# Aggregating and summing layer 1 of a graph network by two groups of four graphs instead of one

## The chip, the cores and the metric

The kernel runs on one core of one Trainium2 chip. Time is measured on the device in microseconds (us), as the median of several runs. Beside these runs there is one execution that the hardware profiler recorded; rows, timelines and waits below come from that one.

Five engines work side by side, each with its own queue of instructions: TensorE (PE in the profile, with its weight loads shown as PEld), VectorE (DVE), ScalarE (ACT), GpSimd (POOL) and SyncE (SP), which here issues transfers only. PSUM is the memory that TensorE writes; VectorE and ScalarE read from it.

## The reference, cut to what matters

128 graphs of 128 nodes with 256 features pass through two layers. Layer 0 is a large gated network (convolutions by a Fourier method, messages between neighbours, gates). Layer 1 looks at the first 25 nodes of each graph only, in five overlapping groups of nodes, 53 rows in all:

```
x = x + layer0(relu(layernorm(x)), adj)
h = relu(layernorm(x))
fused = 0
for g, idx in enumerate(GROUPS):          # sizes 25, 9, 7, 6, 6
    A = adj[:, idx][:, :, idx] + I
    N = D^-1/2 A D^-1/2                   # D: row sums of A
    y = relu(N @ (h[:, idx] @ W1[g]) + b1[g])
    z = relu(N @ (y @ W2[g]) + b2[g])     # this second aggregation is what the change touches
    fused[:, idx] += softmax(fusion_w)[g] * z
x = x + fused
```

Everything is computed in fp32.

## The kernel before, in words

**Layer 0 and its place.** After two batches of preparation, the gates of layer 0 are computed for 32 groups q of four graphs by `stage_c` (products on line 758, some with their own accumulation banks in the pool `pgat`). Each group's result is turned back by VectorE (lines 921 to 939), written to HBM by GpSimd (L941), and read again by `fetch`: the first 32 nodes of the four graphs become `x1`, 128 rows of 256.

**Layer 1 and its tiling.** Layer 1 works in eight blocks of 16 graphs, each block four groups of four (`SB` = 16, `GB` = 4, `QS` = 4). The 53 rows of a graph are padded to 64 (`RP`), so that two graphs fill 128 partitions. For each block:

- `rows` normalizes `x1` of each group.
- `prepare` builds the normalized adjacency `ac` for the 16 graphs (128 partitions: two graphs of 64; eight pairs), and spreads it by one product, `pr4` on L1074, to a mask `r4`. This product stands in the kernel before and is not changed.
- `block` first aggregates (`py`, L1094), then runs the two dense products of the five node groups (`first`, L1111, and `second`, L1120), which end in `yz`, features by rows.
- Then comes the tail of the block, three small functions, each called once for every group q of four graphs. `turn(q)` transposes `yz` back on TensorE into a PSUM bank `pz` (L1142) and ScalarE copies it to `zt`, rows by features for two pairs of graphs (L1146). `gather(q)` aggregates: four products of 64x64 weights with 256 columns, one for each of four graphs, each in its own quadrant of the TensorE array (L1154), into two PSUM tiles `pg2`; VectorE adds the bias to each (L1157), and ScalarE applies relu to both at once (L1158). `fuse(q)` sums the five node groups by two products with 64 weight columns, one on each half of the array's columns (L1164), VectorE adds the result to `x1` (L1166), and the 32 nodes of four graphs are stored. In blocks 0 to 6, GpSimd stores a group with one transfer (L1169). In the last block, each graph has a transfer of its own, 16 in all, issued by SP, but for two of the last group that ScalarE issues (L1173).

**What sets the order.** The order in which instructions enter the queues is written by a planner at build time (`Order`, `Lane`). Programs are Python generators. A step yields two numbers: the time that it is thought to cost, and a pause before the program may go on. Lanes with less work done for their weight go first, if their step is due; otherwise the first lane that is due goes. `stage_c` is one lane; `prepare` and `block` of layer 1 together are another of weight 0.2, two programs at a time. A block begins once its own `prepare` has ended (`P_DONE`) and the gathers of the block before have been issued (`B1_DONE`). In the last products of each layer 0 group the steps of `stage_c` yield a pause of 0.2.

**Buffers.** The pool `ptmp` has five PSUM banks under the tag "tmp" for all short-lived products: those of layer 1 and some of layer 0. A bank holds 512 fp32 columns; a tile of 256 takes a whole bank too. `zt` has four buffers of 2 x 256.

Of the kernel before, what the change touches and what calls it, by code (L numbers as in the profile page):

```python
# [9 lines left out]
FP = mybir.dt.float32  # L10
AF = mybir.ActivationFunctionType
# [4 lines left out]
B, N, D = 128, 128, 256  # L16
# [3 lines left out]
P = 128  # L20
GB = 4
# [9 lines left out]
SB = 16  # L31
QS = SB // GB
NBLK = B // SB
# [7 lines left out]
RP = 64  # L41
WIDE = 32
# [168 lines left out]
def kernel(ctx: ExitStack, tc: tile.TileContext, x, adj, consts, vecs, w_se, conv1_w,  # L211
                    conv2_w, w_msg, b_msg, w_ih, w_hh, W1, W2, b2, fusion_w, out):
    nc = tc.nc
# [7 lines left out]
    ptmp = ctx.enter_context(tc.tile_pool(name="ptmp", bufs=5, space=PSUM))  # L221
# [19 lines left out]
    def v(name, i=None):  # L241
        a, b = VAT[name]
        return vec[:, a:b] if i is None else vec[:, a + i:a + i + 1]
# [17 lines left out]
    s2w = cp.tile([P, 2 * WIDE], FP, name="s2w")  # L261
# [106 lines left out]
    lab, turn = ExitStack(), []  # L368
# [625 lines left out]
    def load_w1(n):  # L994

        if n < NBLK * NG:
            S["w1", n] = S["pool"].tile([P, 2, HID], FP, tag="w1", name=f"w1_{n}", bufs=2)
            nc.sync.dma_start(out=S["w1", n], in_=W1[n % NG].rearrange("(k p) o -> p k o", p=P))
# [83 lines left out]
    def block(blk):  # L1082
        while not (blk in P_DONE and blk - 1 in B1_DONE):
            yield 0.0, 0.5
        pool, yz, b2row = S["pool"], S["yz"], S["b2row"]
        w2, ac, r4 = S["w2"], S["ac"][blk % 2], S["r4"][blk % 2]

        for q in range(QS):
            while blk * QS + q not in R_DONE:
                yield 0.0, 0.5  # L1090
            x1h = S.pop(("x1h", blk * QS + q))
            py = ptmp.tile([P, 2, GB, NR], FP, tag="tmp", name=f"py{blk}_{q}")
            for cc in range(2):
                nc.tensor.matmul(py[:, cc], x1h[:, cc * P:(cc + 1) * P],  # L1094
                                 r4[:, q].rearrange("p j r -> p (j r)"), start=True, stop=True)
            nc.vector.tensor_copy(yz[:, 0, q * GB:(q + 1) * GB, :NR], py[:, 0])  # L1096
            nc.scalar.activation(yz[:, 1, q * GB:(q + 1) * GB, :NR], py[:, 1], AF.Copy)
            PY_DONE.add(blk * QS + q)
            yield 0.75, 0.0 if q < QS - 1 else 2.4

        hs = {}

        def first(g):
            n, o = SIZES[g], OFFS[g]
            w1 = S.pop(("w1", blk * NG + g))
            hh = hs[g] = pool.tile([P, 4, SB, n], FP, tag="hh0" if g == 0 else "hh",
                                   name=f"hh{blk}_{g}", bufs=1 if g == 0 else 2)
            for m in range(4):
                ph = ptmp.tile([P, SB, n], FP, tag="tmp", name=f"ph1{blk}_{g}_{m}")
                for k in range(2):  # L1110
                    nc.tensor.matmul(ph, w1[:, k, m * P:(m + 1) * P],  # L1111
                                     yz[:, k, :, o:o + n], start=(k == 0), stop=(k == 1))
                nc.scalar.activation(hh[:, m], ph, AF.Relu, bias=v("b1", g * 4 + m))  # L1113

        def second(g):
            n, o = SIZES[g], OFFS[g]
            for cc in range(2):
                pz = ptmp.tile([P, SB, n], FP, tag="tmp", name=f"pz1{blk}_{g}_{cc}")
                for m in range(4):
                    nc.tensor.matmul(pz, w2[:, g, m, cc * P:(cc + 1) * P], hs[g][:, m],  # L1120
                                     start=(m == 0), stop=(m == 3))
                nc.vector.tensor_copy(yz[:, cc, :, o:o + n], pz)

        for g in range(NG + 1):
            if g < NG:
                first(g)
                yield 5.5 if g == 0 else 1.95, 0.0
            if g:
                second(g - 1)
                yield 5.5 if g == 1 else 1.95, 0.0 if g < NG else 1.0  # L1130
            if g < NG:
                load_w1(blk * NG + g + 2)
        x1 = X1[blk]

        zts = {}

        def turn(q):
            pz = ptmp.tile([P, 2, D], FP, tag="tmp", name=f"pzt{blk}_{q}")
            for a in range(2):
                for cc in range(2):  # L1140
                    b0 = q * GB + 2 * a
                    nc.tensor.transpose(  # L1142
                        pz[:, a, cc * P:(cc + 1) * P],
                        yz[:, cc, b0:b0 + 2, :].rearrange("p s r -> p (s r)"), ident)
            zt = zts[q] = pool.tile([P, 2, D], FP, tag="zt", name=f"zt{blk}_{q}", bufs=4)
            nc.scalar.activation(zt, pz, AF.Copy)  # L1146

        def gather(q):
            zt = zts[q]
            pg2 = [ptmp.tile([P, D], FP, tag="tmp", name=f"pg2{blk}_{q}_{s}") for s in range(2)]  # L1150
            for a in range(2):
                for s in range(2):
                    rows = slice(s * RP, (s + 1) * RP)
                    nc.tensor.matmul(pg2[s][a * RP:(a + 1) * RP], ac[rows, 2 * q + a],  # L1154
                                     zt[rows, a], start=True, stop=True)
            for s in range(2):
                nc.vector.tensor_add(zt[:, s], pg2[s], b2row)  # L1157
            nc.scalar.activation(zt, zt, AF.Relu)  # L1158

        def fuse(q):  # L1160
            zt = zts.pop(q)
            pf = ptmp.tile([P, D], FP, tag="tmp", name=f"pfu{blk}_{q}")
            for s in range(2):
                nc.tensor.matmul(pf[s * 2 * WIDE:(s + 1) * 2 * WIDE], s2w, zt[:, s],  # L1164
                                 start=True, stop=True)
            nc.vector.tensor_add(x1[:, q], x1[:, q], pf)  # L1166
            b0 = blk * SB + q * GB
            if blk < NBLK - 1:
                nc.gpsimd.dma_start(out=out[b0:b0 + GB, :WIDE], in_=x1[:, q])  # L1169
                return  # L1170
            for j in range(GB):
                eng = nc.scalar if q == QS - 1 and j % 2 else nc.sync
                eng.dma_start(out=out[b0 + j, :WIDE], in_=x1[j * WIDE:(j + 1) * WIDE, q])  # L1173

        for what, q in ((turn, 0), (turn, 1), (turn, 2), (gather, 0), (turn, 3), (gather, 1),
                        (gather, 2), (fuse, 0), (gather, 3), (fuse, 1), (fuse, 2), (fuse, 3)):
            what(q)
            if (what, q) == (gather, QS - 1):
                B1_DONE.add(blk)
            yield {turn: 0.45, gather: 0.5, fuse: 0.5}[what], 0.5  # L1180
        F_DONE.add(blk)


# [23 lines left out]
    loads = Lane([stage_n(q) for q in range(NQ)])  # L1207
    groups = Lane([stage_c(q) for q in range(NQ)], ahead=2)
    second = [setup_1()] + [part(blk) for blk in range(NBLK) for part in (prepare, block)]
    beside.weight = 0.5  # L1210
    order.run(loads, groups, beside, Lane([fetch(q) for q in range(NQ)], ahead=2),
# [43 lines left out]
```

## Time and profile before

| | us |
|---|---|
| median of 3 runs | 1995.26 (1993.5 to 1996.35) |
| profiled execution, its own time | 1999.49 |
| its span, first to last instruction | 1997.7 |
| TensorE busy in the span | 1950.6 |
| VectorE busy | 1349.5 |
| ScalarE busy | 683.2 |
| gather, L1154: 256 records of 128 products, TensorE | 21.4 |
| fuse, L1164: 128 records of 64 products, TensorE | 20.8 |
| bias, L1157: 64 adds of 128x256, VectorE, each | 0.418 |
| relu, L1158: 32 of 128x512, ScalarE, each | 0.630 |
| copy of a turn, L1146: 32 of 128x512, ScalarE, each | 0.593 |
| sum into x1, L1166: 32 adds of 128x256, VectorE, each | 0.417 |
| an add of 128x512 with a broadcast row, L428 (layer 0), each | 0.687 |

How to read it: an fp32 product leaves two records, each with a weight load. Matmuls are pipelined, so a record's duration overlaps the next one's; what a product costs the queue is the distance between starts. A timeline line has the start, the time from the first start to the last end of the instructions merged in it, the engine, the line of the kernel, the operation, output and input, the shape, the count, and in brackets idle time of the engine ahead of it with what ended it.

Layer 1's blocks 0 to 5 run beside layer 0, from about 898 us on. The products of layer 0 end at 1904; its last results are turned until 1917. Blocks 6 and 7 run after that.

### The profile page before, as it was taken

The page shows a single profiled execution, that of the slowest core. Times are in us where ns is not written, and L with a number is a line of the kernel's source. Part 1 is how long each engine was busy: PE and PEld are TensorE (multiplying, and loading weights), DVE is VectorE, ACT ScalarE, POOL GpSimd, SP SyncE. Part 2 cuts the span into 40 slices and gives each one's busy share as a digit, 9 for nine tenths or more (in the row PEclk, how much of TensorE's full clock was granted, in tenths as well). Part 3 has the DMA queues.
Part 4 walks back from the last instruction along what each step waited for, and adds up shares of the span by engine and source line. Part 5 has one row for each costly group of instructions (what it writes and reads, how often), then busy time and mean ns, then how long its engine had stood idle before and what let it go on. Part 6 is the DMA issues. An engine that isn't in the chain of part 4 may idle for free.

```text
span 1997.7 us, 33167 instructions
## 1 busy us (share of the span) xinstructions
PE 1950.6 (98%) x12486; PEld 1610.6 (81%) x12486; DVE 1349.5 (68%) x3042; ACT 683.2 (34%) x1547; POOL 650.1 (33%) x898
## 2 busy tenths in 40 slices
PE   7999999999999999999999999999999999999998
PEld 5667888889888888878778878878888888887865
DVE  6775445875433566885885887778678867886652
ACT  3664222444222344222323322232323322322233
POOL 3553665333665111240321233122221321322320
PEclk9999999999999999999999999999999999999999
DMA  9998778654877643542434343443433533433332
GB/s 207 300 283 274 259 265 283 204 164 152 274 254 254 193 127 106 162 106 80 116 95 108 111 111 84 114 109 95 120 110 82 127 105 98 109 101 98 77 90 57
DMA packets 184106, 302.89 MB, mean 152 GB/s; under 512 B 28501, under 2 KB 131994, under 8 KB 183690
## 3 DMA queue, kind: packets, MB, share of 16 engines
q1 hardware_dynamic: 138762, 168.82, 29.1%
q0 software_dynamic: 44800, 131.66, 23.1%
q8 instruction: 99, 1.62, 0.4%
q14 instruction: 61, 0.50, 0.1%
q10 hardware_dynamic: 384, 0.28, 0.1%
HBM read 204.13 MB, written 109.05 MB: 157 GB/s over the span
## 4 chain that ended last, share of the span: by engine, by line
PE 86%; DVE 6%; DMA 4%; issue 1%; ACT 1%; POOL 1%; SPq 0%; DVEq 0%; POOLq 0%; ACTq 0%
PE p L758 40%; PE pa L534 7%; PE ph L1111 5%; PE pm L645 5%; PE pz L1120 5%; PE pc L425 4%; PE pb L534 3%; PE pf L436 3%; PE px L671 3%; PE pi L715 2%; PE pw L480 1%; PE ph L414 1%; PE py L1094 1%; PE pg L1154 1%; PE pse L629 1%
## 5 line engine op out<-in xcount | busy, mean ns | idle before, releaser
L941 POOL DMA_DIRECT2D x1d<-xt x128 | 101.1, 815 | 418.8 <-DVE xt L939 418.4
L840 POOL DMA_DIRECT2D xt<-in_x x128 | 100.2, 790 | 175.4 <-DMA x1d<-xt 168.3
L566 DVE SCALAR_TENSOR_TENSOR y<-pa,kk 128x512 f32<-128x512 f32 x78 | 53.8, 690 | 151.4 <-ACT kk L565 151.4
L534 PE MATMUL pa<-wf,X 128*128 128x256 f32 x640 | 152.2, 381 | 0.0
L758 PE MATMUL p<-th,wrz 128*128 128x256 f32 x512 | 135.4, 387 | 0.0
L758 PE MATMUL p<-tm,wrz 128*128 128x256 f32 x512 | 131.9, 380 | 0.0
L758 PE MATMUL p<-tc,wrz 128*128 128x256 f32 x512 | 131.4, 379 | 0.0
L534 PEld LDWEIGHTS pa<-wf,X 128*128 128x128 f32 x640 | 118.1, 190 | 16.2 <-issue 2.0
L425 PE MATMUL pc<-c1w,hTa 128*128 128x256 f32 x512 | 121.0, 382 | 1.2 <-ACT hTa L416 1.2
L645 PE MATMUL pm<-wmsg,hT 128*128 128x256 f32 x512 | 121.5, 382 | 0.0
L758 PEld LDWEIGHTS p<-th,wrz 128*128 128x128 f32 x512 | 95.1, 191 | 18.7 <-issue 6.3
L1111 PE MATMUL ph<-yz,w 128*128 128x96 f32 (+3 forms) x640 | 107.9, 322 | 1.8 <-DVE yz L1096 1.3
L758 PEld LDWEIGHTS p<-tm,wrz 128*128 128x128 f32 x512 | 97.8, 191 | 13.5
L425 PEld LDWEIGHTS pc<-c1w,hTa 128*128 128x128 f32 x512 | 94.0, 190 | 18.1 <-DVE h L428 4.8
L758 PEld LDWEIGHTS p<-tc,wrz 128*128 128x128 f32 x512 | 97.3, 190 | 14.0 <-issue 1.0
L645 PEld LDWEIGHTS pm<-wmsg,hT 128*128 128x128 f32 x512 | 95.8, 190 | 15.2 <-ACT kk L565 1.4
L727 ACT ACTIVATE xc<-xc,t_bn 128x256 f32<-128x256 f32 x128 | 58.1, 501 | 145.9 <-DVE xc L724 145.9
L1120 PE MATMUL pz<-hh,w 128*128 128x96 f32 (+3 forms) x640 | 107.3, 322 | 0.0
L1111 PEld LDWEIGHTS ph<-yz,w 128*128 128x128 f32 x640 | 86.8, 190 | 22.9 <-issue 15.0
L1113 ACT ACTIVATE hh<-ph,vec 128x96 f32<-128x96 f32 (+3 forms) x160 | 63.2, 401 | 120.5 <-PE ph L1111 111.7
L1120 PEld LDWEIGHTS pz<-hh,w 128*128 128x128 f32 x640 | 86.3, 191 | 17.6
L758 PE MATMUL p<-hTc,wrz 128*128 128x256 f32 x384 | 99.2, 381 | 1.1 <-DVE z L832 1.1
(207 smaller groups left out, 4433.6 us busy)
## 6 DMA issues: line engine op xcount, KB each, us to landing
wf<-wfd SPq DMA_DIRECT2D x160, 256.0 KB
wfd<-ws POOLq DMA_DIRECT2D x64, 320.0 KB, 9.0
yd<-y POOLq DMA_DIRECT2D x80, 256.0 KB, 4.1
yt<-yd SPq DMA_DIRECT2D x64, 320.0 KB
w<-in_W SPq DMA_DIRECT2D x40, 512.0 KB
xa<-in_x SPq DMA_DIRECT2D x128, 128.0 KB
hTd<-hTa POOLq DMA_DIRECT2D x32, 512.0 KB, 6.7
hT<-hTd SPq DMA_DIRECT2D x32, 512.0 KB
```

The lines of the kernel that those rows point to most:

```text
L425: nc.tensor.matmul(pc[:, i], hT[:, k, (2 * h + i) * N:(2 * h + i + 1) * N], c1w[:, k], start=(k == 0), stop=(k == 1))
L436: nc.tensor.matmul(pf[:, i, :F * NB], h1[:, 2 * h + i, k * P:(k + 1) * P], fwd, start=True, stop=True)
L534: nc.tensor.matmul(ps, xk(k), WF[f][:, k, s], start=(k == 0), stop=(k == 1))
L645: nc.tensor.matmul(pm[:, i], hT[:, k, j * N:(j + 1) * N], LATE["wmsg"][:, k], start=(k == 0), stop=(k == 1))
L671: nc.tensor.matmul(px[:, dc, i], msgs[h][:, i, dc * P:(dc + 1) * P], aT[:, 2 * h + i], start=True, stop=True)
L727: nc.scalar.activation(xc[:, co, s], xc[:, co, s], AF.Relu, bias=sft["bn2"][:, co:co + 1])
L758: nc.tensor.matmul(ps[:, m], w[:, i, k, m * P:(m + 1) * P], factor(i, x, t), start=first and j == 0, stop=last and j == len(n) - 1, skip_g ...
L840: nc.gpsimd.dma_start(out=xt[a * WIDE:(a + 1) * WIDE].rearrange("p b d c -> p (b d) c"), in_=slices(x[q * GB:(q + 1) * GB])[a])
L941: nc.gpsimd.dma_start(out=slices(x1d[q])[a], in_=xt[a * WIDE:(a + 1) * WIDE].rearrange("p b d c -> p (b d) c"))
L1111: nc.tensor.matmul(ph, w1[:, k, m * P:(m + 1) * P], yz[:, k, :, o:o + n], start=(k == 0), stop=(k == 1))
L1113: nc.scalar.activation(hh[:, m], ph, AF.Relu, bias=v("b1", g * 4 + m))
L1120: nc.tensor.matmul(pz, w2[:, g, m, cc * P:(cc + 1) * P], hs[g][:, m], start=(m == 0), stop=(m == 3))
```

## The change

`turn` is still called for each group of four graphs, but writes into a `zt` that holds two groups (two buffers of 2 x 2 x 256). `gather` and `fuse` now take two groups, h: `gather` issues eight quadrant products one after the other into two full PSUM banks, then for each of the two banks an add and a relu of 128x512. `fuse` issues two products of 512 columns, one add to `x1`, and the two groups' stores. The order becomes turn 0, 1, 2, gather 0, turn 3, gather 1, fuse 0, fuse 1. The step of a gather or a fuse is given a cost of 1.0 in place of 0.5, and a gather a pause of 1.5 in place of 0.5. In the last block four of the 16 stores go to ScalarE instead of two.

```diff
@@ turn
-            zt = zts[q] = pool.tile([P, 2, D], FP, tag="zt", name=f"zt{blk}_{q}", bufs=4)
-            nc.scalar.activation(zt, pz, AF.Copy)
-
-        def gather(q):
-            zt = zts[q]
-            pg2 = [ptmp.tile([P, D], FP, tag="tmp", name=f"pg2{blk}_{q}_{s}") for s in range(2)]
-            for a in range(2):
-                for s in range(2):
-                    rows = slice(s * RP, (s + 1) * RP)
-                    nc.tensor.matmul(pg2[s][a * RP:(a + 1) * RP], ac[rows, 2 * q + a],
-                                     zt[rows, a], start=True, stop=True)
+            if q % 2 == 0:
+                zts[q // 2] = pool.tile([P, 2, 2, D], FP, tag="zt", name=f"zt{blk}_{q}", bufs=2)
+            nc.scalar.activation(zts[q // 2][:, q % 2], pz, AF.Copy)
+
+        def gather(h):
+            zt = zts[h]
+            pg2 = [ptmp.tile([P, 2, D], FP, tag="tmp", name=f"pg2{blk}_{h}_{s}")
+                   for s in range(2)]
+            for i in range(2):
+                for a in range(2):
+                    for s in range(2):
+                        rows = slice(s * RP, (s + 1) * RP)
+                        nc.tensor.matmul(pg2[s][a * RP:(a + 1) * RP, i], ac[rows, 4 * h + 2 * i + a],
+                                         zt[rows, i, a], start=True, stop=True)
             for s in range(2):
-                nc.vector.tensor_add(zt[:, s], pg2[s], b2row)
-            nc.scalar.activation(zt, zt, AF.Relu)
-
-        def fuse(q):
-            zt = zts.pop(q)
-            pf = ptmp.tile([P, D], FP, tag="tmp", name=f"pfu{blk}_{q}")
+                nc.vector.tensor_add(zt[:, :, s], pg2[s],
+                                     b2row[:, None, :].to_broadcast([P, 2, D]))
+                nc.scalar.activation(zt[:, :, s], zt[:, :, s], AF.Relu)
+
+        def fuse(h):
+            zt = zts.pop(h)
+            pf = ptmp.tile([P, 2, D], FP, tag="tmp", name=f"pfu{blk}_{h}")
             for s in range(2):
-                nc.tensor.matmul(pf[s * 2 * WIDE:(s + 1) * 2 * WIDE], s2w, zt[:, s],
+                nc.tensor.matmul(pf[s * 2 * WIDE:(s + 1) * 2 * WIDE], s2w, zt[:, :, s],
                                  start=True, stop=True)
-            nc.vector.tensor_add(x1[:, q], x1[:, q], pf)
-            b0 = blk * SB + q * GB
-            if blk < NBLK - 1:
-                nc.gpsimd.dma_start(out=out[b0:b0 + GB, :WIDE], in_=x1[:, q])
-                return
-            for j in range(GB):
-                eng = nc.scalar if q == QS - 1 and j % 2 else nc.sync
-                eng.dma_start(out=out[b0 + j, :WIDE], in_=x1[j * WIDE:(j + 1) * WIDE, q])
+            nc.vector.tensor_add(x1[:, 2 * h:2 * h + 2], x1[:, 2 * h:2 * h + 2], pf)
+            for q in (2 * h, 2 * h + 1):
+                b0 = blk * SB + q * GB
+                if blk < NBLK - 1:
+                    nc.gpsimd.dma_start(out=out[b0:b0 + GB, :WIDE], in_=x1[:, q])
+                    continue
+                for j in range(GB):
+                    eng = nc.scalar if q >= QS - 2 and j % 2 else nc.sync
+                    eng.dma_start(out=out[b0 + j, :WIDE], in_=x1[j * WIDE:(j + 1) * WIDE, q])
 
         for what, q in ((turn, 0), (turn, 1), (turn, 2), (gather, 0), (turn, 3), (gather, 1),
-                        (gather, 2), (fuse, 0), (gather, 3), (fuse, 1), (fuse, 2), (fuse, 3)):
+                        (fuse, 0), (fuse, 1)):
             what(q)
-            if (what, q) == (gather, QS - 1):
+            if (what, q) == (gather, 1):
                 B1_DONE.add(blk)
-            yield {turn: 0.45, gather: 0.5, fuse: 0.5}[what], 0.5
+            yield {turn: 0.45, gather: 1.0, fuse: 1.0}[what], 1.5 if what is gather else 0.5
         F_DONE.add(blk)
```

## The prediction

> **What bounds the kernel.** I read the page first: busy shares, then the chain that ended last.
>
> ```profile
> PE 1950.6 (98%) x12486; PEld 1610.6 (81%) x12486; DVE 1349.5 (68%) x3042; ACT 683.2 (34%) x1547; POOL 650.1 (33%) x898
> PE 86%; DVE 6%; DMA 4%; issue 1%; ACT 1%; POOL 1%; SPq 0%; DVEq 0%; POOLq 0%; ACTq 0%
> ```
>
> TensorE is busy 98% of the span and carries 86% of the chain, so an edit pays where it shortens TensorE's queue or the few places where TensorE waits. In TensorE's timeline I looked at one gather of block 4:
>
> ```profile
> 1717.76 0.60 PE L758 MATMUL p<-tm,wn 128*128 128x256 f32 x2
> 1718.19 0.59 PE L758 MATMUL p<-tc,wn 128*128 128x256 f32 x2
> 1718.72 0.66 PE L1154 MATMUL pg<-zt,ac 64*64 64x256 f32 x8
> 1719.31 0.70 PE L758 MATMUL p<-xm,wn 128*128 128x256 f32 x2
> 1719.85 0.59 PE L758 MATMUL p<-xc,wn 128*128 128x256 f32 x2
> ```
>
> (A product of 256 columns is two records.) Read the starts, since durations overlap. A pair of gate records takes 0.43 us. The gather comes 0.53 after the last pair (0.10 too late), keeps the queue 0.59, and the next pair takes 0.54 (0.11 too long). Its four quadrants stream at once, so 0.43 is streaming: the visit costs 0.80 us, 0.37 of it for entering and leaving. A fuse has starts of the same kind: 0.10 + 0.58 + 0.11 = 0.79. In blocks 0 to 4 all 40 such visits stand alone between other products. Block 5 shows two gathers side by side:
>
> ```profile
> 1903.80 1.09 PE L1154 MATMUL pg<-zt,ac 64*64 64x256 f32 x16
> 1904.82 0.65 PE L1164 MATMUL pfu<-zt,s2w 128*64 128x256 f32 x4
> 1890.00:1917.00 27.00, 23.29 (x137) 15.83 (x136) 20.91 (x54) 10.18 (x21) 8.36 (x12) 1.00 0.30 63
> ```
>
> Sixteen records keep the queue 1.02, against 2 x 0.59 = 1.18 apart. The third line, busy times by stretch (PE, PEld, DVE, ACT, POOL), is where layer 0 ends: TensorE idles 27.00 - 23.29 = 3.71, and VectorE is the limit there.
>
> Last, the end of the span: ScalarE's timeline, TensorE's final fuses, SP's stores.
>
> ```profile
> 1985.67 0.63 ACT L1158 ACTIVATE zt<-zt 128x512 f32<-128x512 f32 x1 [0.82 <-DVE zt L1157]
> 1986.21 0.58 ACT L1146 ACTIVATE zt<-pzt 128x512 f32<-128x512 f32 x1
> 1987.75 1.24 PE L1164 MATMUL pfu<-zt,s2w 128*64 128x256 f32 x8
> 1989.47 0.65 PE L1164 MATMUL pfu<-zt,s2w 128*64 128x256 f32 x4 [0.49 <-ACT zt L1158]
> 1987.91 7.60 SPq L1173 DMA_DIRECT2D out<-x  x14
> ```
>
> The copy of turn 3 (L1146) stands behind the relu of gather 0 (L1158), and SP issues 14 stores without a pause until 1995.5; the span ends 2.2 later. SP's queue sets the end.
>
> **The Trainium skill.** "TensorEngine Tiling (Array Packing)", Key Properties: changing the tiling mode drains TensorE, and tiles run in parallel. The trace agrees: 0.37 us per visit, and four quadrants in the time of one. "TensorE: Matmul & The Clock Gate", Architectural detail: ScalarE and VectorE are strict first-in first-out, TensorE pulls only weight loads ahead; the copy behind the relu agrees. "PSUM — Partial Sum Buffer", The four PSUM rules: one matmul's output fits one bank, 512 fp32 columns; the new 512-column fuse just fits, and L1074 shows such a width (1.02 us for two records).
>
> **The change, part by part.**
> *Gathers.* The same 16 products per block, in two visits for four. From the x16 row: 0.10 + 1.02 + 0.11 = 1.23 for 2 x 0.80, so 0.37 saved per pair.
> *Fuses.* Two visits for four, each of two products of 512 columns on two column halves. No row shows this form. If the halves overlap as at 256 columns: 2 x 0.43 + 0.15 + 0.21 = 1.22 for 2 x 0.79, 0.36 saved. If they didn't, another 0.87, so 0.5 lost per pair; the 256-column row (0.58 for two products that need 0.87 one after the other) excludes that in all likelihood. A gain over 0.36 has no source but the entering cost.
> *Blocks 0 to 4:* 5 x (2 x 0.37 + 2 x 0.36) = -7.3 us, in a queue that has other products ready.
> *VectorE.* Per block 8 adds of 0.418 and 4 of 0.417 (5.0) become 4 + 2 of 128x512, 0.687 by the like row L428 (4.1). The 0.9 saved is hidden under TensorE but where layer 0 ends. ScalarE has the same eight instructions of 128x512.
> *The new wait.* Gather 1 follows turn 3 and its second half needs turn 3's copy, which queues on ScalarE behind both relus of gather 0, and these behind two VectorE adds. From the first gather's end: 0.12 + 2 x 0.66 + 0.09 + 0.63 + 0.58 + 0.05 = 2.8 us. Behind the waiting gather in TensorE's queue stands all of layer 0. In blocks 0 to 5 the planner's pauses (1.5 after a gather, 0.5 after a turn) put two gate steps of 0.87 before turn 3 and one after: 1.74 + 0.44 + 0.87 + 0.6 (gather 1's first half) = 3.65 of cover, 0.85 to spare. VectorE's backlog eats that: in block 4 the adds of the gather at 1715.76 started only at 1718.00, 1.6 us late, behind four copies of L1078. I take 0.2 per block, +1.0 for blocks 0 to 4; bounds 0 and 1 each.
> *Slots.* The starts in TensorE's timeline show how layer 1 gets its turns: about six steps per group of layer 0, in the 0.2 us pauses of its last products (1151.62, 1153.28, 1154.93, 1156.57, 1158.13, 1159.81). A block has 26 steps and 6 of preparation, 190 us at one group per 36.4. After it is 22 and 6, less two slots lost to the 1.5 us pauses: 2 to 4 slots sooner per block. Blocks 0 to 2 wait for data anyhow; blocks 3 to 5 together come 6 to 12 slots, one to two groups, sooner. So block 5's tail falls into layer 0, and block 6's large products stand beside layer 0's end.
> *Block 5 and layer 0's end.* Its visits now cost, by the starts from 1900.84 on, 0.80 + 2.48 + 3 x 0.96 = 6.2; after, 2 x 1.23 + 2 x 1.22 = 4.9: -1.3. Of the 3.71 idle I take 1.1 as recovered (0 to 3): -2.4 in all.
> *Block 6.* Block 7's preparation, sooner by the slots, no longer stands beside its tail, and block 7's own products come only after gather 1, so the new wait is bare (worked out under "the end": 1.55). Turns 1.42, gather 0 1.18, turn 3 0.60, gather 1 0.58 + 1.55 + 0.60, four products py and two fuses with their mode changes 4 x 0.92 + 2 x 1.01 + 5 x 0.2 = 6.7, and 0.5 before the next product: 13.1. Before: 1943.28 to 1956.68, 13.4, less 1.9 of preparation in it (L1069 0.86, L1074 1.05): 11.5. I take +1.5 (-0.2 to 1.8); the preparation itself is only moved.
> *The end.* Gather 0 ends at 1985.13, turn 3 at 1985.72. Adds 1985.25 to 1986.57, relus to 1987.29, copy to 1987.8, gather 1 to 1988.5 (1.55 of wait), fuse 0 to 1989.5. Its add waits behind gather 1's two adds: 1989.95 to 1990.65. SP issues 8 stores from 1990.7 where it began at 1987.9; first two 0.41 + 1.63, others 0.465: 1995.5, the last four to 1997.35 (relu, fuse 1 and its add are done by 1992.45, ScalarE's four stores by 1994.4). With 2.2 of landing, 1999.55: +1.85 (1 to 3).
> *POOL* issues the same 28 stores of 0.69, in pairs; its waits are not on the chain.
> Sum: -7.3 + 1.0 - 2.4 + 1.5 + 1.85 = -5.35. The profiled execution took 1999.49 (span 1997.7), so 1994.1 by its own time; the median of the runs is 1995.26, 4.2 less, so 1989.9.
>
> **Rivals.**
> *A, given back.* Same visits, but the shift of layer 1 recovers nothing at layer 0's end (block 5 -1.3), the wait costs 0.4 per block (+2) and the end +3: -7.3 + 2 - 1.3 + 1.5 + 3 = -2.1, 1993.2. For it: the idle stretch is set by VectorE's order, which I can't derive. Against: by the slots, products that VectorE hardly touches (L1111, L1120) come to stand there.
> *B, slower.* The wait for turn 3's copy opens in each of blocks 0 to 5. It decides for "slower" once it eats the gain and 4 us more: 6.35 (the sum without its 1.0) + 4 = 10.35 over six blocks, 1.73 each, which needs a VectorE backlog of 0.85 + 1.73 = 2.6 us; from 2.6 to 3.2 the time is 1999.3 to 2003. For it: 1.6 was seen, and VectorE is busy 90.76 of 110 us from 1680 to 1790. Against: the 1.6 was behind L1078, which comes once a block, and two adds of 0.69 with a pause left out load VectorE less densely than four times 0.76 in successive pauses.
> *C, more.* Layer 0's end loses nearly all its idle time (another 2), and blocks 0 to 4 don't wait: -5.35 - 2 - 1 = -8.35, 1986.9.
> *D, the fuse doesn't pair:* 16 new fuses at +0.87: -5.35 + 13.9 = +8.6, 2003.8. The overlap seen at 256 columns speaks against it.
>
> **How the numbers follow.** Forecast 0.54 (own range 1987 to 1992), A 0.20, C 0.14, B 0.08, D 0.04. Predicted 1989.9. The range goes from 1984.5, below C with its idle bound of 3 and the end at +1, to 1994.5, above A; left out are B, D and the outer ends, nearly 2 in 10. About 0.2% (4 us) is what a measurement of this kernel can tell from no change, so faster means below 1991.3: of the forecast 0.49, C 0.14, of A 0.07, in all 0.70; same 0.18 (forecast 0.05, A 0.13); slower 0.12 (B, D).
>
> **What will show it.** L1154 in visits of 16 records that keep TensorE's queue about 1.02; L1164 as 64 records of 128x512, four of them about 1.0 to the next start (1.9 would be D). L1157 on VectorE 32 times at 0.69. In blocks 0 to 5, idle time of TensorE or its weight loads before L1154 on ACT L1146: up to 0.4 a block is the forecast, over 1.7 is B. Block 5's fuses begin before 1890, and block 6's first product ph before 1905. From 1890 to 1917, idle below 3. In the last block an L1154 that waits 1.5 us, and the first store 2.8 us later after the last turn than before. Wrong if TensorE's waits in blocks 0 to 5 grow by over 3 us, or if layer 1 gets so far ahead that block 7 waits for the last group's rows.

## The result and the profile after

The changed kernel took 1990.2 us in the median (22 runs, 1987.66 to 1999.2), the kernel before, run beside it, 1999.0 (22 runs, 1993.5 to 2004.56). The ratio is 0.9953, with a 95% interval from 0.9942 to 0.9964. The time lies 0.3 us from the prediction, but that is luck, for two errors meet in it: the first three runs of the kernel before had a median of 1995.26, 3.8 below that of all 22, and the gain was 8.8 us where 5.35 were forecast. A second set of 22 runs of the changed kernel had a median of 1993.23, 6.3 below the kernel before beside it (1999.5). The gain is what has to be explained.

The page of the changed kernel, busy times and the chain that ended last:

```profile
PE 1941.5 (98%) x12422; PEld 1610.1 (81%) x12422; DVE 1344.1 (68%) x2994; ACT 682.3 (34%) x1547; POOL 650.3 (33%) x898
PE 86%; DVE 7%; DMA 4%; issue 1%; ACT 1%; POOL 1%; SPq 0%; DVEq 0%; POOLq 0%; ACTq 0%
```

TensorE is still what bounds the kernel; its busy time fell by 9.1 us with 64 records fewer (by 5.6 in a second profile, which lost 3.4 us more to a lower clock; see below). Next, TensorE's timeline in block 4, a gather of two groups:

```profile
1680.32 0.59 PE L758 MATMUL p<-xc,wn 128*128 128x256 f32 x2
1680.84 1.09 PE L1157 MATMUL pg<-zt,ac 64*64 64x256 f32 x16
1681.87 0.70 PE L758 MATMUL p<-tm,wn 128*128 128x256 f32 x2
1682.40 0.59 PE L758 MATMUL p<-tc,wn 128*128 128x256 f32 x2
```

The visit begins 0.52 after the last gate pair (0.09 too late), keeps the queue 1.03, and the pair after it takes 0.53 (0.10 too long): 1.22 us, forecast 1.23. A fuse costs 1.20, forecast 1.22.

The waits of TensorE from 900 us on (engine, line, what it waited for, us in total, times, longest). The kernel before, then after:

```profile
PE p L758 <- DVE r L880: 4.6, 4, 2.4
PE ph L1111 <- DVE yz L1096: 1.3, 1, 1.3
PE py L1094 <- DVE x L1166: 1.1, 1, 1.1
PE po L902 <- DVE zr L896: 0.9, 1, 0.9
...
PE py L1094 <- DVE zt L1157: 0.4, 1, 0.4
```

```profile
PE p L758 <- DVE r L880: 4.9, 6, 1.4
PE pg L1157 <- ACT zt L1147: 3.0, 3, 1.4
...
PE py L1094 <- DVE r L1078: 0.7, 1, 0.7
```

The four waits at the end of layer 0 (1.3 + 1.1 + 0.9 + 0.4 = 3.7) are gone, and the wait for turn 3's copy has come, in three of eight blocks: 1.03 in block 0, 0.53 in block 6, 1.43 in block 7. Block 6 also has a new wait of 0.7 at its first py. The stretch in which layer 0 ended before now has TensorE busy throughout (columns: stretch, its length, busy TensorE, weight loads, VectorE, ScalarE, GpSimd, then TensorE's granted clock, the share of DMA and GB/s):

```profile
1890.00:1917.00 27.00, 27.00 (x116) 20.48 (x115) 11.48 (x32) 7.24 (x16) 10.16 (x19) 1.00 0.42 98
```

**A steadier measure than the span.** Ahead of block 0's preparation (the first L1069) the program is the same in all kernels of this study, yet in the profiles that part took from 885.9 to 895.0 us, and 885.86 and 890.18 in two profiles of the changed kernel. So the experiments are compared by the stretch from the first L1069 in TensorE's timeline to the end of the span. Before it was 1110.69 us, after 1101.34: 9.35 less. The kernel before has one profile only, so how much its stretch varies isn't known. It falls into four stages:

| stage, by starts in TensorE's timeline | before | after | difference | forecast |
|---|---|---|---|---|
| first L1069 to block 6's second turn | 1056.27 | 1046.18 | -10.09 | -8.7 |
| block 6's second turn to block 7's first L1111 | 13.40 | 13.29 | -0.11 | +1.5 |
| from there to block 7's second turn | 26.01 | 26.22 | +0.21 | 0 |
| from there to the end of the span | 15.01 | 15.65 | +0.64 | +1.85 |

Each start in TensorE's timeline, taken to the next start and less the wait shown at it, gives a ledger by kind of product, good to about 0.1 us. In the first stage the gathers fell by 1.56, the fuses by 2.03, the gate products beside them by 2.98, py by 0.87 and the rest by 0.34, together 7.8; the waits fell by 2.31 (11.93 to 9.62).

### The profile page after: what moved, and what is told of

Read it like the earlier page. It is cut to its first block, busy times and chain, and to the rows that moved or that the text cites. A ratio compares the mean times of both kernels' runs of the same rounds, so it can differ in the third digit from the quotient of the medians.

```text
span 1987.2 us, 32949 instructions
## 1 busy us (share of the span) xinstructions
PE 1941.5 (98%) x12422; PEld 1610.1 (81%) x12422; DVE 1344.1 (68%) x2994; ACT 682.3 (34%) x1547; POOL 650.3 (33%) x898
## 4 chain that ended last, share of the span: by engine, by line
PE 86%; DVE 7%; DMA 4%; issue 1%; ACT 1%; POOL 1%; SPq 0%; DVEq 0%; POOLq 0%; ACTq 0%
PE p L758 39%; PE pa L534 7%; PE ph L1111 5%; PE pm L645 5%; PE pz L1120 5%; PE pc L425 4%; PE pb L534 3%; PE pf L436 3%; PE px L671 3%; PE pi L715 2%; PE ph L414 1%; PE pw L480 1%; PE py L1094 1%; DMA x<-x1d 1%; PE pse L629 1%
## 5 line engine op out<-in xcount | busy, mean ns | idle before, releaser
L1111 PE MATMUL ph<-yz,w 128*128 128x96 f32 (+3 forms) x640 | 108.0, 322 | 0.5 <-issue 0.5
L1111 PEld LDWEIGHTS ph<-yz,w 128*128 128x128 f32 x640 | 86.8, 190 | 21.1 <-issue 16.4
```

Source lines behind the costliest of these rows:

```text
L1111: nc.tensor.matmul(ph, w1[:, k, m * P:(m + 1) * P], yz[:, k, :, o:o + n], start=(k == 0), stop=(k == 1))
```

## The experiments

All eleven kernels are edits of the changed one. "Queue" is the ledger of gathers, fuses and gates, "waits" those of TensorE, both over the whole stretch; "end" is the time from the start of the last row in TensorE's timeline to the end of the span. In the kernels with all turns first (e4 and e6 to e10) that row holds both fuses, 1.2 us more than the last one alone, so their ends compare with one another and not with the rest. "Half" is an estimate of what the stretch lost at half clock, explained below the table.

| kernel | stretch | queue | waits | half | end | ratio of the runs to before [95%] |
|---|---|---|---|---|---|---|
| before | 1110.69 | 776.05 | 13.45 | 0 | 8.23 | |
| changed | 1101.34 | 767.81 | 13.54 | 0 | 8.40 | 0.9953 [0.9942, 0.9964] |
| a1_changed_again | 1100.62 | 767.83 | 12.87 | 0 | 8.44 | 0.9968 [0.9956, 0.998] |
| e1_small_ops | 1100.45 | 767.99 | 13.39 | 0 | 7.89 | 0.9966 [0.9952, 0.998] |
| e2_gather_only | 1105.51 | 772.56 | 12.74 | 0 | 8.12 | 0.9992 [0.9977, 1.0007] |
| e3_late_tail | 1107.82 | 768.12 | 17.31 | 1.7 | 8.42 | 1.0014 [1.0003, 1.0025] |
| e4_turns_first | 1099.36 | 766.96 | 10.56 | 1.7 | 10.12 | 0.9955 [0.9939, 0.9972] |
| e5_stores | 1103.72 | 769.59 | 13.23 | 1.7 | 9.32 | 0.9975 [0.9961, 0.9989] |
| e6_turns_stores | 1099.17 | 766.08 | 10.76 | 0 | 11.19 | 0.9953 [0.9936, 0.9969] |
| e7_one_visit | 1100.22 | 761.97 | 14.29 | 1.7 | 11.59 | 0.9966 [0.9953, 0.9978] |
| e8_even_stores | 1097.53 | 765.96 | 11.71 | 0 | 8.48 | 0.9946 [0.9925, 0.9967] |
| e9_one_visit_late | 1098.53 | 763.58 | 14.84 | 0 | 8.52 | 0.9933 [0.9911, 0.9956] |
| e10_group_stores | 1099.74 | 766.01 | 10.57 | 0 | 11.90 | 0.9947 [0.9927, 0.9968] |

The traces also give the clock that TensorE was granted, as a share of the full one. In four profiles it falls to half for 3.4 us within the stretch: in e3, e7, e5 and e4, here in this order, with the columns of the line above (the granted clock is the third figure from the end):

```profile
1920.50:1923.90 3.40, 3.40 (x6) 1.68 (x5) 2.65 (x12) 0.59 (x1) 2.24 (x8) 0.50 0.29 79
1943.20:1946.60 3.40, 3.40 (x10) 2.80 (x12) 3.19 (x9) 2.74 (x5) 0.23 (x1) 0.50 0.00 0
1658.90:1662.20 3.30, 3.30 (x9) 2.61 (x8) 2.32 (x8) 1.75 (x3) 0.00 (x0) 0.50 0.48 159
1054.40:1057.70 3.30, 3.30 (x9) 2.88 (x10) 0.38 (x1) 0.87 (x3) 0.00 (x0) 0.50 0.00 0
```

By estimate each costs half its length, 1.7 us. No wait is shown for it, since the products just take longer: the ledger has 1.7 more in e3's L1111 and in e5's gates, products that the edits leave as they are. The other profiles, the one of the kernel before included, have none in the stretch until TensorE's last product is done.

**The changed kernel once more** (no edit).

> The changed kernel itself, once more. The stretch from the first product of L1069 to the end of the span, where alone the two kernels differ, took 1110.7 us before and 1101.3 in the changed kernel. If this stretch is steady and the spread of the runs comes from the part ahead of it, it takes 1100.8 to 1101.8 again, while the start of L1069 moves by up to some us (885.9 in the first profile, 895.0 in the kernel with the late tail).

The stretch came within 0.72 us of the first one while the part ahead of it moved by 4.3. About 0.7 us is thus what two profiles without half clock can differ by (the gates' waits for VectorE at L880 come out differently), and a difference below that is not read as anything. The ratios of the runs carry the unsteady part too: two sets of 22 runs of one kernel gave 0.9953 and 0.9968.

**The merged visits with the small instructions.** TensorE's order and the steps are those of the changed kernel, but the fuse has four products of 256 columns and VectorE its adds of 256.

```diff
-                nc.vector.tensor_add(zt[:, :, s], pg2[s],
-                                     b2row[:, None, :].to_broadcast([P, 2, D]))
-                nc.scalar.activation(zt[:, :, s], zt[:, :, s], AF.Relu)
+            for i in range(2):
+                for s in range(2):
+                    nc.vector.tensor_add(zt[:, i, s], pg2[s][:, i], b2row)
+                nc.scalar.activation(zt[:, i], zt[:, i], AF.Relu)
...
-                nc.tensor.matmul(pf[s * 2 * WIDE:(s + 1) * 2 * WIDE], s2w, zt[:, :, s],
-                                 start=True, stop=True)
-            nc.vector.tensor_add(x1[:, 2 * h:2 * h + 2], x1[:, 2 * h:2 * h + 2], pf)
+                    nc.tensor.matmul(pf[s * 2 * WIDE:(s + 1) * 2 * WIDE, i], s2w, zt[:, i, s],
+                                     start=True, stop=True)
+            for i in range(2):
+                nc.vector.tensor_add(x1[:, 2 * h + i], x1[:, 2 * h + i], pf[:, i])
```

> The order of TensorE's products and the planner's steps are those of the changed kernel, but every fuse is four products of 256 columns again, the bias and x1 adds are of 128x256 again (8 and 4 per block), and a relu covers one group. If the gain comes from the number of visits of the tiled modes, L1157 and the fuse cost TensorE's queue as in the changed kernel (about 1.21 us a visit) and the time is that of the changed kernel within 2 us, ratio to before 0.995 to 0.9965. If the larger instructions of VectorE and ScalarE bring a good part of it, 3 us or more are lost, ratio 0.997 or above.

The stretch was 1100.45, between 0.2 and 0.9 below the two profiles of the changed kernel, and gathers and fuses cost the same to 0.2 us. Wider instructions bring nothing by themselves here; what saves time is that fewer visits are made.

**The gathers merged, the fuses apart**, each fuse with its own step, one group at a time.

```diff
-        def fuse(h):
-            zt = zts.pop(h)
-            pf = ptmp.tile([P, 2, D], FP, tag="tmp", name=f"pfu{blk}_{h}")
+        def fuse(q):
+            zt = zts[q // 2]
+            pf = ptmp.tile([P, D], FP, tag="tmp", name=f"pfu{blk}_{q}")
...
-                        (fuse, 0), (fuse, 1)):
+                        (fuse, 0), (fuse, 1), (fuse, 2), (fuse, 3)):
...
-            yield {turn: 0.45, gather: 1.0, fuse: 1.0}[what], 1.5 if what is gather else 0.5
+            yield {turn: 0.45, gather: 1.0, fuse: 0.5}[what], 1.5 if what is gather else 0.5
```

> Gathers of two groups as in the changed kernel, fuses of one group each in steps of their own as before. Theory of visits: 16 fuse visits more than in the changed kernel, of which 10 to 12 stand alone between full-array products at 0.35 us each: 3.5 to 4.2 us slower than the changed kernel, ratio about 0.997; the gathers' own share of about 4 us stays. If the number of visits doesn't matter (the gain is only the moved tail of block 5), the time stays at the changed kernel's, 0.9953, as long as block 5's tail lies before layer 0's end.

The stretch was 4.2 us longer than the changed kernel's. The ledger puts it where a count of visits does: the fuses cost 2.29 more, the gates beside them 2.53, the waits 0.8 less. The prediction had put the merging of the fuses in blocks 0 to 4 at 5 x 0.72 = 3.6. The runs agree on the side and show rather more: a ratio of 0.9992 against 0.9953 and 0.9968 is 5 to 8 us.

**The tail of block 5 held back** by empty steps of the planner; all instructions stay.

```diff
+        for _ in range(14 if blk == 5 else 0):
+            yield 0.0, 0.5
         for what, q in ((turn, 0), (turn, 1), (turn, 2), (gather, 0), (turn, 3), (gather, 1),
```

> The changed kernel with 14 empty planner steps ahead of block 5's turns, so that block 5's tail stands at the end of layer 0 again, as it does in the kernel before. If the idle time there (3.7 us before, 0 in the changed kernel) was a gain of its own, about 3 us come back: ratio 0.9965 to 0.997, and TensorE idles 2.5 us or more in the 12 us after layer 0's last product. If the idle time is only traded for waits elsewhere, the time stays within 1 us of the changed kernel, 0.995.

The stretch was 6.5 us longer than the changed kernel's, twice what was expected; 1.7 of that are half clock, which leaves 4.8. TensorE's waits around layer 0's end in this kernel:

```profile
PE po L902 <- DVE zr L896: 2.6, 1, 2.6
PE pg L1157 <- ACT zt L1147: 0.9, 1, 0.9
PE ph L1111 <- DVE yz L1096: 0.8, 1, 0.8
```

Its stretch of 13 us there has TensorE busy for 8.75:

```profile
1906.90:1920.00 13.10, 8.75 (x51) 4.82 (x50) 10.37 (x25) 5.39 (x12) 2.94 (x5) 1.00 0.08 17
```

With the same visits, the waits alone are up by 3.8 over the changed kernel. So the place of block 5's tail is a gain of its own, of about the size of the 3.7 us of idle time seen before. The starts of L1111 took 1.7 more: the half clock from 1920.5 on, right behind these waits. The last us lies in py (+0.65) and small rows; its cause stays open. By the runs the kernel lost more, 9 to 12 us against the changed one. The mean granted clock of its 22 runs was 0.9954, that of the two sets of the changed kernel 0.9979 and 0.9972; by estimate that is 4 to 5 us of it.

**All four turns ahead of the gathers.**

```diff
-        for what, q in ((turn, 0), (turn, 1), (turn, 2), (gather, 0), (turn, 3), (gather, 1),
+        for what, q in ((turn, 0), (turn, 1), (turn, 2), (turn, 3), (gather, 0), (gather, 1),
```

> The changed kernel with turn 3 ahead of gather 0 in every block, so that ScalarE's copy of turn 3 no longer queues behind the relus of gather 0. If the three waits of the gather on that copy (1.03, 0.53 and 1.43 us in blocks 0, 6 and 7) are time lost, they go and the kernel is 2 to 3 us faster than the changed one, ratio 0.9938 to 0.9945. If another wait takes their place (VectorE's adds before the fuse, SP's stores), less than 1 us is gained, 0.995.

All three waits of L1157 on the copy are gone and the waits fell from 13.54 to 10.56: the copy stood behind the relus, as the prediction said. The stretch fell by 2.0 only because 1.7 went to half clock at 1054, in gates and a py that the edit doesn't touch; without it, 3.7. From block 7's second turn to the end of the span it was 14.5 in place of 15.65. In the timeline of its end (start, length, engine, line), the fuses follow each other and SP still has twelve stores to issue:

```profile
1981.18 2.87 PE L1168 MATMUL pfu<-zt,s2w 128*64 128x512 f32 x8 [0.67 <-ACT zt L1162]
...
1983.61 5.46 SPq L1178 DMA_DIRECT2D out<-x  x12
```

**The last block's first two groups stored by GpSimd**, one transfer each, first alone and then with the turns ahead.

```diff
-                if blk < NBLK - 1:
+                if blk < NBLK - 1 or h == 0:
```

> The changed kernel, but in the last block the first two groups are stored by GpSimd with one transfer each, so that SP issues 4 stores and not 12. If SP's queue sets the end, the span ends 2.2 us after SP's or ScalarE's last issue near 1983.1 by the changed kernel's clock, and 1.8 to 2.0 us are gained. If the landing of the stores sets it, or GpSimd's transfers take over (4.7 us to land in the median), the gain is below 1 us.

> Turn 3 ahead of gather 0 and the two GpSimd stores together. Turns first alone took the stretch from 1101.3 to 1099.4, its end after TensorE's last product being 1.7 longer. If SP's queue gave that back, both together give 1.6 to 2.5 more: 1096.9 to 1097.8 from L1069 to the end, ratio to before 0.9935. If the two gains overlap, 1098.5 or more.

Alone, the edit made the stretch 2.4 us longer. Of that, 1.7 are the half clock at 1659, in gates that the edit doesn't touch; what the edit did is the end, longer by 0.9. With the turns ahead (1099.17) the end was 11.19, longer than e4's 10.12; the stretch came out the same only because e4 has the half clock and this one has not. The end of the first:

```profile
1987.59 1.44 POOL L1174 DMA_DIRECT2D out<-x  x2 [21.86 <-DVE x L1170]
1988.81 1.76 SPq L1178 DMA_DIRECT2D out<-x  x4
```

SP's four stores are issued by 1990.57 and the span ends at 1995.7. GpSimd's two were issued by 1989.03, 6.7 us before the end. In the changed kernel SP's last issue ends 2.2 us before the end of the span. So moving stores to GpSimd exchanged a queue of issues for a slower landing.

**The sixteen stores shared evenly by SP and ScalarE**, with the turns ahead.

```diff
-                    eng = nc.scalar if q >= QS - 2 and j % 2 else nc.sync
+                    eng = nc.scalar if j % 2 else nc.sync
```

> Turn 3 ahead of gather 0, and the last block's 16 stores given in turn to SP and ScalarE, 8 each. With turns first alone the end (TensorE's last product to the end of the span) took 10.12 us, SP issuing 12 stores from 2.4 us after that product on. If SP's queue sets the end, 4 stores fewer at 0.46 give 1.7 to 1.9 us: end 8.2 to 8.5, and 1097.3 to 1097.8 from L1069 to the end of the span. If ScalarE's issues delay its relus or the landing sets the end, less than 0.7 is gained.

Both queues are done together:

```profile
1980.85 3.63 SPq L1178 DMA_DIRECT2D out<-x  x8
1980.85 3.70 ACTq L1178 DMA_DIRECT2D out<-x  x8
```

The end fell from e4's 10.12 to 8.48: SP's count of issues had set the end. That the stretch fell by as much, 1.8 to 1097.53, is chance: e4's half clock (1.7) is gone, and block 7's L1111 waited 1.1 for a transfer of weights, which e4 didn't. This is the shortest stretch of all, 3.1 to 3.8 below the two profiles of the changed kernel. The runs (1990.95; 0.9946 against 0.9953) can't separate the two: the difference is below what they resolve.

**The same with one transfer of 128 KB per group.**

```diff
-                for j in range(GB):
-                    eng = nc.scalar if q >= QS - 2 and j % 2 else nc.sync
-                    eng.dma_start(out=out[b0 + j, :WIDE], in_=x1[j * WIDE:(j + 1) * WIDE, q])
+                eng = nc.scalar if q % 2 else nc.sync
+                eng.dma_start(out=out[b0:b0 + GB, :WIDE], in_=x1[:, q])
```

> As the kernel with turns first and even stores, but a group of four graphs is stored with one transfer of 128 KB, two from SP and two from ScalarE. If the number of issues sets the end, two per queue leave it free at once and the end is the last add's end plus one issue and landing, 1.5 us or more shorter than with even stores. If one large transfer takes longer to land than four small ones, that is lost again, and the end is equal or longer.

```profile
1984.53 1.75 SPq L1177 DMA_DIRECT2D out<-x  x2
1984.53 2.09 ACTq L1177 DMA_DIRECT2D out<-x  x2
```

The queues are done by 1986.62, but the span ends at 1994.0, 7.4 later; the end is 11.90, the longest of all. The Trainium skill, "DMA: Bandwidth & Descriptors", Rules for kernel authors, advises to coalesce many small transfers into a large one. At the end of this span the measurement says otherwise: with sixteen stores of 32 KB the span ended 3.4 us sooner after TensorE's last row than with four of 128 KB. The runs of the two (0.9946 and 0.9947) can't tell them apart, and the two kernels don't separate a store's size from its form (32 or 128 partitions).

**Both gathers in one step, both fuses in one step**, first on e6, then on e8 with three empty steps after each in blocks 0 to 5.

```diff
-        for what, q in ((turn, 0), (turn, 1), (turn, 2), (gather, 0), (turn, 3), (gather, 1),
-                        (fuse, 0), (fuse, 1)):
-            what(q)
-            if (what, q) == (gather, 1):
+        for what, qs in ((turn, (0,)), (turn, (1,)), (turn, (2,)), (turn, (3,)), (gather, (0, 1)),
+                         (fuse, (0, 1))):
+            for q in qs:
+                what(q)
+            if what is gather:
...
-            yield {turn: 0.45, gather: 1.0, fuse: 1.0}[what], 1.5 if what is gather else 0.5
+            yield {turn: 0.45, gather: 2.0, fuse: 2.0}[what], 1.5 if what is gather else 0.5
```

What e9 has besides, after that step:

```diff
+            for _ in range(3 if what is not turn and blk < NBLK - 2 else 0):
+                yield 0.0, 0.5
```

> As the kernel with turns first and GpSimd stores, with both gathers of a block in one step and both fuses in one step: two visits of the tiled modes fewer per block and two planner steps fewer. Theory of visits: 12 visits fewer in blocks 0 to 5 at 0.35 us, 4.2 us less than that kernel for the rows of gather, fuse and gates together. Theory of the slots: layer 1 gets so far ahead that block 6's tail stands at layer 0's end and block 7's products py wait for the last group's rows, with VectorE the limit there: 4 us or more of TensorE's idle time near layer 0's end, and the total is no better than that of the kernel with turns first and GpSimd stores.

> As the kernel with turns first and even stores, with both gathers and both fuses of a block in one step each (two visits fewer per block), and three empty planner steps after each of the two in blocks 0 to 5, so that layer 1 runs no further ahead than in the changed kernel and block 6's large products stand at layer 0's end. Theory: visits and the place of the tail are independent. The rows of gather, fuse and gates stay 4 us below the kernel with even stores, as in the kernel with one visit, and TensorE's waits near layer 0's end, 4.2 us there, fall below 1.5: 1093 to 1094.5 from L1069 to the end. If waits for PSUM banks or VectorE's four adds in a row take the gain, 1096 or more.

In e7 the queue fell by 4.1 us against e6, 0.34 for each of the twelve visits saved in blocks 0 to 5, yet the stretch grew by 1.05: the waits grew by 3.5, and 1.7 went to the half clock from 1943.2 on, right behind the first of these waits (from 1930 to 1955):

```profile
PE po L902 <- DVE zr L896: 2.5, 1, 2.5
PE py L1094 <- ACT x1h L1015: 1.3, 1, 1.3
```

Layer 1 had come so far ahead that a py waited for the rows of the last group. In e9, with layer 1 held back, the waits near layer 0's end were down to 0.9 in all, but of the queue only 2.4 us were won against e8, and 3.1 of new waits took that: the gates waited for VectorE elsewhere.

```profile
PE p L758 <- DVE r L880: 5.2, 7, 1.8
...
PE p L758 <- DVE r L872: 1.8, 3, 1.0
```

The stretch was 1.0 longer than e8's, near what two profiles differ by, and its runs had the lowest median (1989.56; 0.9933, six runs). Which of e8 and e9 is better is left open; by the stretch both are below the changed kernel.

## Why the prediction was right and where it was not

**Right: the visits.** In blocks 0 to 4, 40 lone visits with 0.34 to 0.44 us above streaming became 20 with the same, at 1.20 to 1.30 each; the forecast took 1.23 and 1.22. With what the gates beside them took above 0.43 a pair, these visits fell from 32.0 to 24.7 us, 7.4 less, where 7.3 were forecast. The two products of 512 columns of a fuse do overlap, so rival D falls; e1 and e2 show this gain to come from the count of visits and not from wider instructions. The Trainium skill, "TensorEngine Tiling (Array Packing)", Key Properties, says that a change of mode drains the array. A cost of 0.35 us per visit, whatever its length, fits that; no run here separates the draining from other costs of a visit, the first weight loads for one. Over blocks 0 to 5 the rows fell by 7.8 in place of 8.6, so the miss lies in block 5 and what stands beside it. The -0.87 that py contributes to that was not in the sum: before, block 5's fuses stood between the py of block 6, and a py costs 0.91 beside such a visit and 0.72 beside gates.

**Right in size, wrong in spread: the new wait in blocks 0 to 4.** Forecast 0.2 in each of five blocks, 1.0; measured 1.03 in block 0 and nothing in blocks 1 to 5. Rival B, which needed 1.73 in each, falls. Blocks 0 to 4 thus came to about the -6.3 forecast.

**Wrong in size: layer 0's end.** The step said that of 3.71 us of idle time 1.1 would be recovered, with 3 as the bound. All 3.7 went, which was rival C's mechanism. The reason given (block 5's tail a group or two earlier, so that block 6's large products stand there) held: block 5's fuses came at 1869.29 and 1872.94, block 6's first L1111 at 1901.90, each inside its mark. VectorE, 20.91 us busy in the stretch from 1890 to 1917 before, had 11.48 after. With TensorE fully fed there, there was no reason to keep 2.6 us of idle; the discount was the error. e3 is the counter-test: the same visits with the tail late cost 4.8 us, besides the half clock.

**Wrong: block 6, +1.5.** The step that failed is that block 7's preparation "no longer stands beside its tail" and leaves the wait bare. The timeline of the changed kernel has it there:

```profile
1932.86 1.02 PE L1069 MATMUL pg<-dd,cst 128*128 128x512 f32 x2
...
1934.25 1.09 PE L1157 MATMUL pg<-zt,ac 64*64 64x256 f32 x16
1935.27 1.13 PE L1074 MATMUL pr<-ac,cst 128*128 128x512 f32 x2
1936.24 0.60 PE L1142 MATMUL pzt<-cst,yz 128*128 128x128 f32 x4
1936.77 0.66 PE L1157 MATMUL pg<-zt,ac 64*64 64x256 f32 x8
1937.96 0.66 PE L1157 MATMUL pg<-zt,ac 64*64 64x256 f32 x8 [0.53 <-ACT zt L1147]
```

L1074 between the first gather and turn 3 covers 1.0 us of the copy's delay, and 0.53 is left of 1.55. In both kernels L1069 follows block 6's turns: the preparation moved with block 6, not apart from it. That is 1.0 of the 1.6 us by which the forecast missed. The rest is a term that was too large: four py and two fuses were put at 6.7 and took 5.5. The sum added five changes of mode at 0.2 to a py of 0.92, but those 0.92 were measured beside visits and held the change already (0.72 beside gates). Against that stands the wait of 0.67 for VectorE (L1078) at the first py, which the sum didn't have.

**Wrong in size: the end, +1.85.** The wait was as forecast (1.43 for 1.55). The timelines of ScalarE, TensorE and SP:

```profile
1974.84 1.23 ACT L1162 ACTIVATE zt<-zt 128x512 f32<-128x512 f32 x2 [1.13 <-DVE zt L1160]
1975.98 0.58 ACT L1147 ACTIVATE zt<-pzt 128x512 f32<-128x512 f32 x1
1976.61 0.66 PE L1157 MATMUL pg<-zt,ac 64*64 64x256 f32 x8 [1.43 <-ACT zt L1147]
...
1979.30 5.73 SPq L1178 DMA_DIRECT2D out<-x  x12
```

The first store came 2.5 us later after the second turn than before (7.75 against 5.22; forecast 2.8). But the prediction carried over one slow issue of the profile of before (1.59 us for one of SP's fourteen, among others of about 0.42), and none of the twelve took more than 0.43: they were issued in 5.73 us where the sum had 6.7. With the 0.3 of the first store that is the 1.2 us by which the forecast missed; the last stage grew by 0.64. What had been a single long record was taken for a property of the queue.

In sum: of the 4.0 us that the stretch gained beyond the forecast, 1.4 come before block 6's turns (2.6 more idle time recovered, some of it lost again in rows and other waits), 1.6 in block 6, 1.2 at the end, and 0.2 go the other way in block 7. Rival A, which let layer 0's end give nothing back, falls by the idle time, though the second set of runs (1993.23) lay at its time. Rival C's gain (8.35) came nearest to that of the stretch, with one of its two grounds: the idle time went, but the wait in blocks 0 to 4 didn't.

## What to carry to other kernels

Where small tiled products stand between full-size ones, count the visits: each cost 0.35 us beside its streaming, and wider instructions in the same number of visits brought nothing. Then ask where a planner's saved slots put the tail of the work, since that was worth about 4 us more here, and can turn into waits when the consumer gets too far ahead of its producer (e7). Before a difference of one or two us is put down to an edit, look at the granted clock in both profiles. At the end of a span, count the issues on each queue and how late each kind of transfer lands, and don't carry over a single long record as a cost.

## What the runs showed of the hardware that was not expected

A wait of TensorE can cost more than its length. In each of the four profiles above, TensorE was busy for less than half of the 3.4 us ahead of the half clock (1.48 of the 3.50 us to 1920.5 in e3, 0.51 of the 3.40 to 1943.2 in e7). Not every such wait is followed by one: the changed kernel waited 2.0 us at the same py as e4 (1.96) and kept its clock. The two kernels that waited 2.5 us or more at layer 0's end, e3 and e7, have the lowest mean granted clock of all, 0.9954 and 0.9956 over 22 runs each. That the waits are the cause is likely and not shown.

The spread of the runs goes with the clock. Of the 65 runs of the kernel before that stood beside a1, the twelve with a mean granted clock of 0.996 took 2002.1 us on average, the six with 0.999 took 1995.3.

The part ahead of block 0, the same program in all kernels, took 885.9 to 895.0 us. A visible piece of it is TensorE's wait at L660 for a transfer: 2.0 us before, 2.4 after, 3.0 in a1 and 5.1 in e3. Behind the last two the clock fell to half, behind the first two it didn't. In this whole part half clock cost, by half its length, 1.7 us before and after and 5.1 in a1, which is by estimate 3.4 of the 4.3 between the two profiles of the changed kernel. Why the transfers run at a different pace from one execution to the next is open.

At the end of the span, stores of 32 KB from SP or ScalarE, each issued in about 0.42 us, let the span end 2.2 to 2.4 us after the last issue where no larger store was under way; two of 128 KB from GpSimd 6.7 to 7.5 after, and 128 KB ones from SP and ScalarE 7.4 after.
